# One level of Strassen or two: a float32 factorization kernel on one NeuronCore

## The chip, the core and the metric

The kernel runs on one NeuronCore of one Trainium2 chip. The engines are TensorE (PE in the profile; its weight loads are PEld), VectorE (DVE), ScalarE (ACT), GpSimd (POOL) and SyncE (SP, which here only starts transfers). They work through separate queues, each in order, and wait for one another through semaphores. The metric is device microseconds (us) of the whole program. "The profile" is one execution taken by the hardware profiler; "the page" is its printed summary.

## The reference

`x` is 1024 x 512, the weight is 64 x 512 x 512 (e, f, m), all float32:

```python
out_lin = x @ lin_w.T + lin_b
xv = jnp.einsum('bf,efm->bem', x, weight)
zp = jnp.einsum('bf,efm->bem', jnp.square(x), jnp.square(weight))
interaction = 0.5 * jnp.sum(jnp.square(xv) - zp, axis=1)
return out_lin + interaction
```

The large part is `xv`: a 1024 x 512 matrix times a 512 x 32768 one, of which only the squares, summed over e, are kept. `zp` summed over e needs only the sum over e of the squared weight, one 512 x 512 matrix (`w2_sum`), and one small matrix product.

## The kernel before

The host lays the weight out as 64 column blocks of 512 columns, each with 8 output columns m and all 64 e, so that the sum over e is a sum over 64 neighbours. A block is a 128 x 4 x 512 tile (`w`, 1 MB): 128 partitions, four slices of the contracted dimension.

The kernel multiplies with one level of Strassen (in Winograd's form). The row blocks of `x` and the two halves of the contracted dimension make a 2 x 2 left matrix, `A11` to `A22`; two neighbouring column blocks make the 2 x 2 right matrix. The left sums `S1` to `S4` are made once. For each pair of blocks `column_sums` makes four right sums `t1` to `t4` on VectorE (L124 to L127). Seven products take the place of eight. A product (`product`, L143) is 2 row tiles of 128 rows (`G = 2`) times 2 slices of 128, four matmuls of 128 x 128 by 128 x 512, into a PSUM tile of two banks.

The loop runs over 64 trees: 32 pairs of blocks times two row pieces. The order is written out by hand (`manual_schedule`): products 1, 3, 6, 2, 7, then product 5 of the next tree, then 4. There are four PSUM tiles: `b1`, two `b2`, `b3`. Partial results go on in PSUM: product 1 is copied from `b1` to a `b2` by ScalarE, and products 6, 7 and 4 are added onto it in that bank by TensorE; product 5 is copied out of `b3` as `p5` before product 3 is added onto it, and the sum is copied out as `p53`. Two results need `p53` or `p5` added, by VectorE (L204, L212). Each of the four results of a tree is squared by ScalarE and summed over e by VectorE into `acc` (`finish`, L155 and L156). `squares` (L132, L133) does the same to the weight for `w2_sum`.

All weight loads are on SP's queue. At the start eight matmuls of zeros keep TensorE busy while the first transfers run. At the end, 64 matmuls (L247) make the linear term and the squares' term together, and VectorE adds `acc` and the bias (L252, L255) before the stores.

Of the kernel before, what the change touches and what calls it, by code (L numbers as in the profile page):

```python
# [8 lines left out]
F32 = mybir.dt.float32  # L9
AF = mybir.ActivationFunctionType  # L10
ALU = mybir.AluOpType
AX = mybir.AxisListType


@with_exitstack
def kernel(
# [24 lines left out]

    nc = tc.nc
    NBLK, P, NK, N = weight.shape
    B = xT.shape[1]
    M = out.shape[1]
    MI = M // NBLK
    E = N // MI
    NB = B // P
    H = B // 2
    G = 2  # L50
    NT = H // (G * P)

    const = ctx.enter_context(tc.tile_pool(name="const", bufs=1))
    wpool = ctx.enter_context(tc.tile_pool(name="wpool", bufs=4))
    tpool = ctx.enter_context(tc.tile_pool(name="tpool", bufs=2))
    w2pool = ctx.enter_context(tc.tile_pool(name="w2pool", bufs=1))
    ppool = ctx.enter_context(tc.tile_pool(name="ppool", bufs=2))
    sqpool = ctx.enter_context(tc.tile_pool(name="sqpool", bufs=3))
    opool = ctx.enter_context(tc.tile_pool(name="opool", bufs=2))
    ps1 = ctx.enter_context(  # L60
        tc.tile_pool(name="ps1", bufs=1, space=bass.MemoryType.PSUM)
    )
    ps2 = ctx.enter_context(
        tc.tile_pool(name="ps2", bufs=2, space=bass.MemoryType.PSUM)
    )
    ps3 = ctx.enter_context(
        tc.tile_pool(name="ps3", bufs=1, space=bass.MemoryType.PSUM)
    )
    ctx.enter_context(tc.manual_schedule())

    def psum_tile(kind, name):
        pool = {1: ps1, 2: ps2, 3: ps3}[kind]
        return pool.tile([P, G, N], F32, tag=f"b{kind}", name=f"b{kind}_{name}")

    zero = sqpool.tile([P, N], F32, tag="sq", name="zero")
    nc.vector.memset(zero, 0.0)
    for kind in (1, 2, 2, 3):
        b = psum_tile(kind, f"prime{kind}")
        for j in range(G):
            nc.tensor.matmul(b[:, j, :], zero[:, 0:P], zero, start=True, stop=True)  # L80

    x_src = xT.rearrange("(p k) b -> p k b", k=NK)
    KH = NK // 2

    def const_half(tag):
        return const.tile([P, KH, H], F32, tag=tag, name=tag)

    A = {}
    for h, k, queue in ((0, 0, nc.scalar), (1, 0, nc.scalar), (1, 1, nc.sync), (0, 1, nc.scalar)):
        a = A[h, k] = const_half(f"a{h}{k}")  # L90
        queue.dma_start(a, x_src[:, ts(k, KH), ts(h, H)])

        if (h, k) == (0, 0):
            blocks = {}

            def load(c):
                w = blocks[c] = wpool.tile([P, NK, N], F32, tag="w", name=f"w{c}")
                if c < 2:
                    for q in range(2):
                        nc.sync.dma_start(w[:, ts(q, KH), :], weight[c][:, ts(q, KH), :])  # L100
                else:
                    nc.sync.dma_start(w, weight[c])

            load(0)
            load(1)

    A11, A12, A21, A22 = A[0, 0], A[0, 1], A[1, 0], A[1, 1]
    S1, S2, S3, S4 = (const_half(f"s{i}") for i in range(1, 5))
    lhs = {1: A11, 2: A12, 3: S4, 4: A22, 5: S1, 6: S2, 7: S3}

    acc = const.tile([P, NB, M], F32, tag="acc", name="acc")
    w2_sum = const.tile([P, NK, M], F32, tag="w2_sum", name="w2_sum")

    def column_sums(n):

        w0, w1 = blocks[2 * n], blocks[2 * n + 1]
        b11, b21, b12, b22 = (
            w0[:, 0:KH, :], w0[:, KH:NK, :], w1[:, 0:KH, :], w1[:, KH:NK, :]
        )
        t = {  # L120
            i: tpool.tile([P, KH, N], F32, tag=f"t{i}", name=f"t{i}_{n}")
            for i in range(1, 5)
        }
        nc.vector.tensor_sub(t[1], b12, b11)  # L124
        nc.vector.tensor_sub(t[2], b22, t[1])  # L125
        nc.vector.tensor_sub(t[3], b22, b12)  # L126
        nc.vector.tensor_sub(t[4], b21, t[2])  # L127
        return {1: b11, 2: b21, 3: b22, 4: t[4], 5: t[1], 6: t[2], 7: t[3]}

    def squares(c):  # L130
        w2 = w2pool.tile([P, NK, N], F32, tag="w2", name=f"w2_{c}")
        nc.scalar.activation(w2, blocks[c], AF.Square)  # L132
        nc.vector.tensor_reduce(  # L133
            w2_sum[:, :, ts(c, MI)],
            w2.rearrange("p k (m e) -> p k m e", e=E),
            axis=AX.X,
            op=ALU.add,
        )

    def product(i, rhs, t, b, first):  # L140
        for j in range(G):
            for k in range(KH):
                nc.tensor.matmul(  # L143
                    b[:, j, :],
                    lhs[i][:, k, ts(t * G + j, P)],
                    rhs[i][:, k, :],
                    start=first and k == 0,
                    stop=k == KH - 1,
                    skip_group_check=True,
                )  # L150

    def finish(c, src, h, t, name):

        sq = sqpool.tile([P, G, N], F32, tag="sq", name=f"sq{name}")
        nc.scalar.activation(sq, src, AF.Square)  # L155
        nc.vector.tensor_reduce(  # L156
            acc[:, h * (NB // 2) + t * G:h * (NB // 2) + (t + 1) * G, ts(c, MI)],
            sq.rearrange("p j (m e) -> p j m e", e=E),
            axis=AX.X,
            op=ALU.add,  # L160
        )

    trees = [(n, t) for n in range(NBLK // 2) for t in range(NT)]
    rhs_of = {}
    live = {}

    def open_tree(s):
        n, t = trees[s]
        b3 = psum_tile(3, s)
        product(5, rhs_of[n], t, b3, True)  # L170
        p5 = ppool.tile([P, G, N], F32, tag="p5", name=f"p5_{s}")
        nc.scalar.copy(p5, b3)  # L172
        live[s] = b3, p5

    for s, (n, t) in enumerate(trees):
        name = f"{n}_{t}"
        if s == 0:
            b1 = psum_tile(1, s)
            nc.vector.tensor_sub(S3, A11, A21)
            nc.vector.tensor_add(S1, A21, A22)  # L180
            rhs_of[0] = column_sums(0)
            product(1, rhs_of[0], t, b1, True)
            nc.vector.tensor_sub(S2, S1, A11)
            nc.vector.tensor_sub(S4, A12, S2)
            open_tree(0)
        if t == 0 and n + 1 < NBLK // 2:
            load(2 * n + 2)
            load(2 * n + 3)
        rhs = rhs_of[n]
        b3, p5 = live.pop(s)  # L190

        if s > 0:
            b1 = psum_tile(1, s)
            product(1, rhs, t, b1, True)
        b2 = psum_tile(2, s)
        nc.scalar.copy(b2, b1)  # L196

        product(3, rhs, t, b3, False)
        p53 = ppool.tile([P, G, N], F32, tag="p53", name=f"p53_{s}")
        nc.scalar.copy(p53, b3)  # L200

        product(6, rhs, t, b2, False)
        c12 = ppool.tile([P, G, N], F32, tag="c12", name=f"c12_{s}")
        nc.vector.tensor_add(c12, b2, p53)  # L204

        product(2, rhs, t, b1, False)
        finish(2 * n, b1, 0, t, f"11_{s}")
        finish(2 * n + 1, c12, 0, t, f"12_{s}")

        product(7, rhs, t, b2, False)  # L210
        c22 = ppool.tile([P, G, N], F32, tag="c22", name=f"c22_{s}")
        nc.vector.tensor_add(c22, b2, p5)  # L212
        finish(2 * n + 1, c22, 1, t, f"22_{s}")

        if t == 0:
            squares(2 * n)
            squares(2 * n + 1)
            if n + 1 < NBLK // 2:
                rhs_of[n + 1] = column_sums(n + 1)
        if s + 1 < len(trees):  # L220
            open_tree(s + 1)
        product(4, rhs, t, b2, False)
        finish(2 * n, b2, 1, t, f"21_{s}")

        if s == 1:
            lw_sb = const.tile([P, NK, M], F32, tag="lw", name="lw_sb")
            bias_sb = const.tile([P, M], F32, tag="bias", name="bias_sb")
            nc.gpsimd.dma_start(lw_sb, lin_wT.rearrange("(p k) m -> p k m", k=NK))
            nc.gpsimd.dma_start(bias_sb, lin_b.partition_broadcast(P))
        if s == 3:  # L230
            xq = {}
            for hk, a in A.items():
                xq[hk] = const_half("xq%d%d" % hk)
                nc.vector.scalar_tensor_tensor(xq[hk], a, -0.5, a, ALU.mult, ALU.mult)

    out_dst = out.rearrange("(n p) m -> p n m", p=P)
    kinds = (2, 1, 3, 2)
    for g in range(NB // G):
        ps = psum_tile(kinds[g], f"out{g}")
        o = opool.tile([P, G, M], F32, tag="o", name=f"o{g}")  # L240
        h = g // NT
# [44 lines left out]
```

## Time and profile before

| | |
|---|---|
| median of 3 runs | 1625.71 us (1625.59 to 1626.24) |
| profiled execution | 1625.93 us, its span from first to last instruction 1624.2 us |
| granted TensorE clock | 0.997 |
| TensorE matmuls busy | 1606.1 us, 3728 instructions |
| VectorE / ScalarE / GpSimd busy | 774.5 / 565.7 / 1.4 us |
| HBM traffic | 70.52 MB read, 2.10 MB written |

A busy share is the time in which an engine had an instruction running, over the span. In the page's groups a row names the line, the engine, the operation and the tiles it writes and reads, then the busy time, the mean ns of one instruction, the idle time of the engine just before them and what ended it. "The chain that ended last" goes back from the last instruction to whatever released it, and so on to the start.

### The profile page before, as it was taken

The page shows a single profiled execution, that of the slowest core. Times are in us where ns is not written, and L with a number is a line of the kernel's source. Part 1 is how long each engine was busy: PE and PEld are TensorE (multiplying, and loading weights), DVE is VectorE, ACT ScalarE, POOL GpSimd, SP SyncE. Part 2 cuts the span into 40 slices and gives each one's busy share as a digit, 9 for nine tenths or more (in the row PEclk, how much of TensorE's full clock was granted, in tenths as well). Part 3 has the DMA queues.
Part 4 walks back from the last instruction along what each step waited for, and adds up shares of the span by engine and source line. Part 5 has one row for each costly group of instructions (what it writes and reads, how often), then busy time and mean ns, then how long its engine had stood idle before and what let it go on. Part 6 is the DMA issues. An engine that isn't in the chain of part 4 may idle for free.

```text
span 1624.2 us, 9096 instructions
## 1 busy us (share of the span) xinstructions
PE 1606.1 (99%) x3728; PEld 709.4 (44%) x3728; DVE 774.5 (48%) x601; ACT 565.7 (35%) x513; POOL 1.4 (0%) x6
## 2 busy tenths in 40 slices
PE   7999999999999999999999999999999999999998
PEld 3444444444444444444444444444444444444433
DVE  3556444455444455543445544445544444554421
ACT  1333333343343333333333334333333333333410
POOL 0000000000000000000000000000000000000000
PEclk9999999999999999999999999999999999999999
DMA  4111001111001111101111100111100111110001
GB/s 187 52 52 52 21 31 52 52 52 52 26 26 52 52 52 52 44 19 41 52 52 52 52 26 26 52 52 52 52 34 21 48 52 52 52 52 0 0 13 39
DMA packets 12009, 73.19 MB, mean 45 GB/s; under 512 B 1280, under 2 KB 1280, under 8 KB 3904
## 3 DMA queue, kind: packets, MB, share of 16 engines
q1 hardware_dynamic: 10928, 69.74, 12.0%
q10 hardware_dynamic: 816, 1.57, 0.3%
q0 software_dynamic: 224, 1.31, 0.2%
q8 instruction: 29, 0.48, 0.1%
q14 instruction: 12, 0.10, 0.0%
HBM read 70.52 MB, written 2.10 MB: 45 GB/s over the span
## 4 chain that ended last, share of the span: by engine, by line
PE 98%; DMA 1%; DVE 0%; SPq 0%; issue 0%; ACT 0%; DVEq 0%
PE b L143 95%; PE b_out L247 3%; DMA a<-xT 1%; DVE o L252 0%; SPq L100 0%; DVE c L212 0%; DVE t L124 0%; ACT p L172 0%; DVE o L255 0%; DVE s L180 0%; DVEq L125 0%
## 5 line engine op out<-in xcount | busy, mean ns | idle before, releaser
L143 PE MATMUL b<-t,s 128*128 128x512 f32 x1536 | 682.7, 594 | 6.6 <-DVE t L124 6.6
L156 DVE TENSOR_REDUCE acc<-sq 128x16 f32<-128x1024 f32 x256 | 306.0, 1216 | 419.0 <-ACT sq L155 419.0
L143 PE MATMUL b<-w,a 128*128 128x512 f32 x1024 | 460.3, 592 | 0.0
L143 PEld LDWEIGHTS b<-t,s 128*128 128x128 f32 x1536 | 292.8, 191 | 375.7 <-issue 375.7
L143 PEld LDWEIGHTS b<-w,a 128*128 128x128 f32 x1024 | 194.6, 190 | 244.9 <-issue 244.9
L155 ACT ACTIVATE sq<-b 128x1024 f32<-128x1024 f32 x128 | 131.1, 1024 | 456.1 <-PE b L143 456.1
L143 PE MATMUL b<-t,a 128*128 128x512 f32 x512 | 230.3, 592 | 1.3 <-DVE c L212 1.3
L143 PE MATMUL b<-w,s 128*128 128x512 f32 x512 | 230.3, 592 | 1.1 <-ACT p L172 1.1
L204 DVE TENSOR_TENSOR c<-b,p 128x1024 f32<-128x1024 f32 x64 | 78.3, 1224 | 280.4 <-PE b L143 275.1
L155 ACT ACTIVATE sq<-c 128x1024 f32<-128x1024 f32 x128 | 134.7, 1053 | 176.6 <-DVE c L212 176.6
L133 DVE TENSOR_REDUCE w_sum<-w 128x32 f32<-128x2048 f32 x64 | 146.3, 2286 | 81.8 <-ACT w L132 81.8
L143 PEld LDWEIGHTS b<-t,a 128*128 128x128 f32 x512 | 97.2, 190 | 124.1 <-issue 122.0
L143 PEld LDWEIGHTS b<-w,s 128*128 128x128 f32 x512 | 97.2, 190 | 123.9 <-issue 122.0
L132 ACT ACTIVATE w<-w 128x2048 f32<-128x2048 f32 x64 | 121.7, 1902 | 75.3 <-DVE w_sum L133 75.3
L200 ACT COPY p<-b 128x1024 f32<-128x1024 f32 x64 | 64.8, 1013 | 156.4 <-PE b L143 156.4
L196 ACT COPY b<-b 128x1024 f32<-128x1024 f32 x64 | 63.8, 997 | 74.1 <-PE b L143 72.9
L172 ACT COPY p<-b 128x1024 f32<-128x1024 f32 x64 | 64.1, 1002 | 55.3 <-PE b L143 55.3
L212 DVE TENSOR_TENSOR c<-b,p 128x1024 f32<-128x1024 f32 x64 | 78.4, 1225 | 1.1
L125 DVE TENSOR_TENSOR t<-w,t 128x1024 f32<-128x1024 f32 x32 | 39.2, 1225 | 1.1
L126 DVE TENSOR_TENSOR t<-w 128x1024 f32<-128x1024 f32 x32 | 39.0, 1219 | 0.0
L127 DVE TENSOR_TENSOR t<-w,t 128x1024 f32<-128x1024 f32 x32 | 39.0, 1218 | 0.0
L124 DVE TENSOR_TENSOR t<-w,w 128x1024 f32<-128x1024 f32 x32 | 38.9, 1216 | 0.0
(21 smaller groups left out, 118.2 us busy)
## 6 DMA issues: line engine op xcount, KB each, us to landing
w<-weight SPq DMA_DIRECT2D x62, 1024.0 KB, 4.8
w<-weight SPq DMA_DIRECT2D x4, 512.0 KB, 10.7
out<-o SPq DMA_DIRECT2D x8, 256.0 KB, 2.0
a<-xT ACTq DMA_DIRECT2D x3, 512.0 KB, 12.6
lw_sb<-lin_wT POOLq DMA_DIRECT2D x1, 1024.0 KB, 10.2
a<-xT SPq DMA_DIRECT2D x1, 512.0 KB, 14.8
bias_sb<-lin_b POOLq DMA_DIRECT2D x1, 256.0 KB, 11.5
```

The lines of the kernel that those rows point to most:

```text
L125: nc.vector.tensor_sub(t[2], b22, t[1])
L132: nc.scalar.activation(w2, blocks[c], AF.Square)
L133: nc.vector.tensor_reduce(w2_sum[:, :, ts(c, MI)], w2.rearrange("p k (m e) -> p k m e", e=E), axis=AX.X, op=ALU.add,)
L143: nc.tensor.matmul(b[:, j, :], lhs[i][:, k, ts(t * G + j, P)], rhs[i][:, k, :], start=first and k == 0, stop=k == KH - 1, skip_group_check ...
L155: nc.scalar.activation(sq, src, AF.Square)
L156: nc.vector.tensor_reduce(acc[:, h * (NB // 2) + t * G:h * (NB // 2) + (t + 1) * G, ts(c, MI)], sq.rearrange("p j (m e) -> p j m e", e=E), ...
L172: nc.scalar.copy(p5, b3)
L196: nc.scalar.copy(b2, b1)
L200: nc.scalar.copy(p53, b3)
L204: nc.vector.tensor_add(c12, b2, p53)
L212: nc.vector.tensor_add(c22, b2, p5)
L247: nc.tensor.matmul(ps[:, j, :], lo[h, k // KH][:, k % KH, bt], hi[:, k, :], start=(q == 0), stop=(q == 2 * NK - 1),)
```

## The change

The right matrix now has four column blocks (a group; 16 groups), and Strassen is used twice. The outer level takes the group as 2 x 2 quarters of 256 x 1024 (`w11`, `w12`, `w21`, `w22`, 1 MB each) and the left matrix as four quarters of 512 x 256. The inner level splits each of the seven outer products again. That gives 49 products of 256 x 128 by 128 x 512, two matmuls each, where the kernel before needs 56 products of that size.

- *Left sums.* The seven outer left operands and their inner sums are made once, in `X[1]` to `X[7]`, seven pieces each.
- *Right sums.* The four outer sums of a group (`outer_sum`: `T1`, `T2`, and two written over `w12` and `w21`) are made by VectorE on 2048 columns. The four inner sums of each outer product (`inner_t`) are made by GpSimd on 512 columns.
- *Inner results* are collected in PSUM as before (`b1`, `b2`, `b3`).
- *Outer results* are collected in SBUF tiles (`O1`, `U2`, `U3`), by VectorE as each PSUM tile is read (`outer_psum`, `outer_sbuf`). Where `p5` or `p53` enters too, GpSimd first adds the collected sum to it (`before_sum`). The outer product 5 goes into two results, and there GpSimd does two additions to `U3` and `U2` for each SBUF result.
- *Order.* A tree is one outer product; each group runs its trees in the order 1, 6, 2, 7, 4, 5, 3. Within a tree the inner order is product 1, product 4 of the tree before, 6, 5 of the next tree, 2, 7, 3 of the next tree. The sums over e are put in a queue (`defer`) and emitted in `end_slot` while the VectorE backlog that the program reckons is under a limit; squares are emitted some slots after their result (`at`).
- *Ends.* The linear term is computed first and put in DRAM; each group's partial `acc` goes to DRAM; both come back in the last trees into the weight tiles, which are free then. The priming matmuls are gone. At the end 32 matmuls make the squares' term.

The core of the changed code (the diff replaces nearly the whole body of the kernel function):

```diff
+ORDER = (1, 6, 2, 7, 4, 5, 3)
+SLOT = {1: 0, 7: 1, 2: 2, 4: 3, 5: 4, 6: 5, 3: 6}
...
+    def outer_sum(g, which):
+        t = tiles[g]
+        if which == 1:
+            t["T1"] = full_tile(wpool, "T1", f"T1_{g}")
+            nc.vector.tensor_sub(t["T1"], t["w12"], t["w11"])
+        elif which == 2:
+            t["T2"] = full_tile(wpool, "T2", f"T2_{g}")
+            nc.vector.tensor_sub(t["T2"], t["w22"], t["T1"])
+        elif which == 3:
+            nc.vector.tensor_sub(t["w12"], t["w22"], t["w12"])
+        else:
+            nc.vector.tensor_sub(t["w21"], t["w21"], t["T2"])
+        spend(2.3)
...
+    def inner_t(s, which):
...
+        new = t[which] = tpool.tile([P, N], F32, tag=f"t{which}", name=f"t{which}_{s}")
...
+        nc.gpsimd.tensor_sub(new, a, b)
...
+    def end_slot(limit=1.0):
+        now[0] += 1
+        for fn in later.pop(now[0], ()):
+            fn()
+        while deferred and deferred[0][0] <= now[0]:
+            ready, cost, fn = deferred[0]
+            if busy["dve"] > now[0] + limit and now[0] < ready + 12:
+                break
+            deferred.popleft()
+            spend(cost)
+            fn()
...
+    def product(s, p, b, first):
+        i = trees[s][1]
+        r = rhs(s, p)
+        for j in range(G):
+            nc.tensor.matmul(
+                b[:, j, :], X[i][:, SLOT[p], ts(j, P)], r,
+                start=first, stop=True, skip_group_check=True,
+            )
...
+    def outer_psum(s, b, pos):
+        i = trees[s][1]
+        if i == 1:
+            nc.scalar.copy(target(s, i, pos), b)
+        elif i == 5:
+            nc.vector.tensor_add(U3[pos], U3[pos], b)
+            nc.vector.tensor_add(U2[pos], U2[pos], b)
+            spend(2.44)
+            finish(s, U3[pos], pos, 2)
+        else:
+            other = addend(i, pos)
+            t = target(s, i, pos)
+            nc.vector.tensor_add(t, b, other)
+            spend(1.22)
+            if i in (2, 4, 3):
+                finish(s, t, pos, 2)
+
+    def before_sum(s, p, pos):
+        i = trees[s][1]
+        if i not in (1, 5):
+            nc.gpsimd.tensor_add(p, p, addend(i, pos))
+
+    def outer_sbuf(s, b, p, pos):
+        i = trees[s][1]
+        spend(1.22)
+        if i == 5:
+            nc.vector.tensor_add(p, b, p)
+            nc.gpsimd.tensor_add(U3[pos], U3[pos], p)
+            nc.gpsimd.tensor_add(U2[pos], U2[pos], p)
+            finish(s, U3[pos], pos, 4)
+        else:
+            t = target(s, i, pos)
+            nc.vector.tensor_add(t, b, p)
+            if i in (2, 4, 3):
+                finish(s, t, pos, 2)
...
+    for s in range(last + 1):
+        g, idx = divmod(s, 7)
+        more = g + 1 < NG
+        if s < last:
+            b1s[s] = bank(1, s)
+            product(s, 1, b1s[s], True)
+            b2s[s] = bank(2, s)
+            nc.scalar.copy(b2s[s], b1s[s])
+            before_sum(s, p5[s], 3)
...
+            if idx == 6 and more:
+                outer_sum(g + 1, 2)
+            end_slot()
+        if s > 0:
+            product(s - 1, 4, b2s[s - 1], False)
+            outer_psum(s - 1, b2s[s - 1], 2)
...
+        inner_t(s + 1, 2)
...
+        if idx == 1:
+            outer_sum(g, 3)
+        end_slot()
+        product(s, 6, b2s[s], False)
+        outer_sbuf(s, b2s[s], p53[s], 1)
+        end_slot()
+        first_half(s + 1)
+        inner_t(s + 1, 3)
...
+        end_slot()
+        product(s, 2, b1s[s], False)
+        outer_psum(s, b1s[s], 0)
+        inner_t(s + 1, 4)
...
+        end_slot()
+        product(s, 7, b2s[s], False)
+        outer_sbuf(s, b2s[s], p5[s], 3)
+        if idx == 2:
+            outer_sum(g, 4)
+        if idx == 5 and more:
+            outer_sum(g + 1, 1)
+        end_slot()
+        second_half(s + 1)
+        if s + 1 < last:
+            before_sum(s + 1, p53[s + 1], 1)
+        inner_t(s + 2, 1)
+        end_slot()
```

`first_half(s)` is product 5 into `b3` and ScalarE's copy of it to `p5`; `second_half(s)` is product 3 onto the same bank and the copy to `p53`. `finish` squares a result in place on ScalarE and puts its sum over e in the queue. `spend(c)` is the program's own reckoning of VectorE's time in slots and issues nothing. The loads of the next group's quarters are on SP's queue in the trees with idx 0 (`w22`), 1 (`w11`), 4 (`w12`) and 5 (`w21`).

## The prediction

> **What bounds the kernel now.** I read the page first for busy shares and the chain that ended last, then the chain in order of time for what surrounds the loop, then the groups for prices. The page:
>
> ```profile
> span 1624.2 us, 9096 instructions
> ...
> PE 1606.1 (99%) x3728; PEld 709.4 (44%) x3728; DVE 774.5 (48%) x601; ACT 565.7 (35%) x513; POOL 1.4 (0%) x6
> ...
> PE 98%; DMA 1%; DVE 0%; SPq 0%; issue 0%; ACT 0%; DVEq 0%
> ```
>
> TensorE is on 98% of the chain; VectorE and ScalarE have half their time free, GpSimd does nothing. The chain in order of time:
>
> ```profile
> 20.20 6.14 PE b L143 x8
> ...
> 27.43 1528.11 PE b L143 x3560
> ...
> 1556.85 3.70 PE b L143 x8
> 1560.55 6.88 PE b_out L247 x16
> ```
>
> The second line is one unbroken run: 1528.11/3560 = **0.4292 us per TensorE instruction**. One float32 matmul is two instructions (1792 matmuls in the products, 3584 instructions), so it costs 0.858 us. Everything outside the products: 27.4 us before the long run, less 8 instructions already done, and 63.7 us from 1560.55 to the end, of which 128 x 0.429 = 54.9 is matmul. Prices of the other engines, from the costliest groups:
>
> ```profile
> L156 DVE TENSOR_REDUCE acc<-sq 128x16 f32<-128x1024 f32 x256 | 306.0, 1216 | 419.0 <-ACT sq L155 419.0
> L204 DVE TENSOR_TENSOR c<-b,p 128x1024 f32<-128x1024 f32 x64 | 78.3, 1224 | 280.4 <-PE b L143 275.1
> L133 DVE TENSOR_REDUCE w_sum<-w 128x32 f32<-128x2048 f32 x64 | 146.3, 2286 | 81.8 <-ACT w L132 81.8
> L200 ACT COPY p<-b 128x1024 f32<-128x1024 f32 x64 | 64.8, 1013 | 156.4 <-PE b L143 156.4
> ```
>
> The first row squares' sums, the second adds a PSUM bank to an SBUF tile: both 1.22 us for 1024 columns; 2048 columns take 2.29; a ScalarE pass takes 1.0.
>
> **What the Trainium skill says.** (1) "GPSIMD Engine Reference", section 3.1, measures a float32 tensor_tensor add of 2048 columns at 4497 ns on GpSimd and 2293 on VectorE, about 2.6 cycles of 1.2 GHz per element. The VectorE side agrees with 2286 above; nothing in this trace shows GpSimd arithmetic. (2) "SBUF — State Buffer", section "Who interferes with whom": a VectorE instruction with two SBUF inputs contends with a GpSimd instruction that reads SBUF; with one SBUF input (the other in PSUM, or a reduce) it does not. Not shown here. (3) "TensorE: Matmul & The Clock Gate", Part 1: after an idle window of about 3.4 us TensorE runs at half clock until a busy window has passed. The trace agrees: after a wait of 6.6 us the eight instructions at 20.20 took 6.14 us, where eight warm ones take 3.43.
>
> **The change, part by part.** I call one product (two matmuls, 4 instructions) a slot: 4 x 0.4292 = 1.717 us. A tree is 7 slots (12.02 us), a group of four column blocks 49 slots (84.1 us), and there are 16 groups.
>
> *TensorE.* 64 block products become 49: 16 x 49 x 4 = 3136 instructions x 0.4292 = 1346.1 us, against 3584 and 1538.4: **minus 192.3**. The linear term (32 matmuls, 27.5 us) moves from the end to the start; the squares' matmuls (27.5) stay at the end; the 8 priming matmuls go.
>
> *Start.* The first matmul needs three transfers of 256 KB; at the 346 GB/s that the trace shows in its first 20 us, shared with others in flight, some 5 us. The clock is cold then: plus 2. Linear matmuls 27.5, under which 7 MB arrive (7/0.346 = 20 us), so loads are hidden. Then ScalarE copies stand between products of the first tree with no other tree to cover them (product 5 to 3, product 1 to 6): 1.2 and 1.4 us. First product effectively at 5 + 2 + 27.5 + 2.6 = 37.1 (before: 1560.55 - 1538.4 = 22.1). *End.* 27.5 of matmul, four banks free, then one addition of 0.69 us and the store (3.1 us behind the last VectorE instruction now): 31.3. The 30 small reloads of partial sums on SP's queue start a tree and a half earlier and have that and 27 us; I cost them at nothing, and at 10 if they are late. Floor: 37.1 + 1346.1 + 31.3 = **1414.5** with nothing late.
>
> *VectorE per group.* 28 additions from PSUM x 1.224 = 34.3, 24 reduces x 1.216 = 29.2, 4 outer sums of 2048 columns x 2.29 = 9.2: 72.6 of 84.1 us (86%). Each addition must end before the bank is written again, mostly two slots after: 3.43 us, less 1.4 of its own. The reduces are held back by the emission rule while its reckoned backlog is over one slot. The first group has 28 small sums more (some 10 us) and is full. *ScalarE per group.* 21 copies, 2 more in the first tree, 24 squares: 47 x about 1.02 = 48 us. Where a square lies between the copies after product 3 and product 1: 0.2 + 3 x 0.95 = 3.1 us against the 3.43 at which product 6 is due: fits by 0.3.
>
> *GpSimd per group.* By (1), 60 ns and 2.17 ns a column: 1.17 us for 512 columns, 2.28 for 1024. 28 inner sums = 32.8; 10 additions to p5 or p53 and 4 for tree 5 = 31.9: 64.7 of 84.1. In an ordinary tree its tightest deadline is the inner sum T1 of the next tree: product 3 ends, copy 0.2 + 1.0, addition to p53 2.28, T1 1.17: 4.7 us against the 5.15 (three slots) at which product 5 is due. It fits, with 0.45 to spare.
>
> *Where it does not fit: tree 5 to tree 3.* Time from the start of tree 5. Product 6 ends at 5.15, VectorE's addition at 6.6. GpSimd adds to U3 and U2: 11.15; the two inner sums queued behind: 13.5; the second pair of additions, ready at 12.3: 18.05; the addition to p53 of tree 3: 20.35; T1 of the next group's first tree: 21.5. That T1 is due at 12.02 + 5.15 = 17.17. **TensorE waits 4.35 us**, with every engine's later work behind it. In the same stretch VectorE makes the next group's first two outer sums (4.6 us, two SBUF inputs). By (2) they contend. Full exclusion adds 4.6: 8.9. Shared by the cycle, GpSimd reads two operands in 2.6 cycles (8.0 us of work hold 6.2 of the port), VectorE reads one operand per 0.96 GHz cycle (3.7): 9.9 instead of 8.0, so 6.2 late. I take **6.2**, between 4.35 and 8.9. By (3) a wait over 3.4 us tends to cool the clock: 0.6, **1.8**, 2.7 for the three (the trace's 2.7 as the top, scaled by how surely an idle window falls in the wait). The last group has no successor: 15 x (6.2 + 1.8) = **120 us**.
>
> *Small lateness elsewhere* (outer sum 4 just before T1 of tree 4, ScalarE's 0.3 us): 0 to 2 us per group; I take 0.5: 8.
>
> *SP's queue:* four 1 MB loads per group (4.8 us each) against 84 us; the shortest lead, for w12, is eight slots, 13.7 us. Nothing, while that lead stands. The sums' stores to DRAM wait for the last reduce and hold the next load behind them by a few slots: not due for several trees.
>
> Sum: 1414.5 + 120 + 8 = 1542.5 of span. The execution profiled took 1625.93 for a span of 1624.2, 1.7 more, and lies 0.2 above the median: **1544 us**.
>
> **The rivals.**
> *Slower: the shared port covers the PSUM additions too.* If the one SBUF operand of those 28 additions also comes through the interface that GpSimd uses, 64.7 + 9.2 + 34.3 = 108.2 us per group cannot overlap: 16 x 108.2 + 68.4 = 1800. It decides once the exclusive time passes (1624.2 - 68.4)/16 = 97.2 us a group, that is when 68% of the additions' time is shut out. Against it: the skill's page names two SBUF inputs only. For it: no run here has shown GpSimd reading at all, and the priced work sits at 77% and 86% of two engines side by side.
> *All hidden.* GpSimd is a fifth faster than the page (the 14.9 us from 6.6 to 21.5 shrink to 11.9, 1.4 late) and ports do not collide: 1414.5 + 21 + 1.7 = 1437; with no wait 1416.
> *VectorE becomes the bound.* At 86% by plan, in order, with outer sums of 2.3 us ahead of additions that have 2 us of slack, a bank is late in most trees: 1 us in each of 112 trees on top of 1544 gives some 1650 without recovery, 1600 with half recovered.
> *It does not do what it says:* the compiled order of TensorE has 1568 product matmuls and 64 others, so that is ruled out.
>
> **How the numbers follow.** GpSimd late at each group's end, with contention from none (1414.5 + 15 x 4.95 = 1489) to full (1414.5 + 15 x 11.6 + 16 = 1604): 0.65. All hidden: 0.15. VectorE bound: 0.06. Port covers PSUM additions: 0.14. The range 1425 to 1615 takes the first wholly and most of the second and third. Faster 0.65 + 0.15 + 0.03 = 0.83, slower 0.14 + 0.02 = 0.16, between them 0.01; 0.2% is about what a measurement of this kernel can tell from no change.
>
> **What would show it.** Right: TensorE's product rows busy 1346 us at 0.429 each; GpSimd rows at 1.17 and 2.28 us; among the waits, product instructions on GpSimd's t, longest 5 to 9 us, some 15 times, each followed by a few instructions at half pace; outer sums stretched beyond 2.3 us. Wrong: GpSimd rows far from the page's price; product waits spread over all trees and put down to VectorE (the third rival); VectorE's PSUM additions at 2 us or more in place of 1.22 (the first); a tail over 45 us after the last product (the reloads).

## The result, and the profile after

The changed kernel takes **1674.62 us** (median of 4 runs, 1673.40 to 1675.18) where the kernel before takes 1625.65 (4 runs, 1625.02 to 1626.24): the ratio is 1.03 (95% interval 1.0282 to 1.0318). It is 3% slower; 1544 us and faster had been forecast, with a range that ended at 1615.

The page of the kernel after, its busy shares, the chain that ended last, and the costliest groups (columns as before; "issue" is time in which an engine on the chain waited for nothing that the profile shows):

```profile
span 1672.9 us, 10435 instructions
...
PE 1472.8 (88%) x3264; PEld 634.9 (38%) x3264; DVE 1207.1 (72%) x950; ACT 748.8 (45%) x756; POOL 1187.0 (71%) x677
...
PE 36%; POOL 33%; issue 27%; DVE 3%; ACT 1%; DMA 0%; POOLq 0%; DVEq 0%; SPq 0%
...
L271 PE MATMUL b<-t,X 128*128 128x512 f32 x1792 | 851.1, 614 | 176.6 <-POOL t L238 169.5
...
L345 POOL TENSOR_TENSOR p<-p,oa 128x1024 f32<-128x1024 f32 x96 | 226.9, 2364 | 203.8 <-ACT p L375 203.8
...
L353 POOL TENSOR_TENSOR oa<-oa,p 128x1024 f32<-128x1024 f32 x32 | 106.0, 3313 | 88.6 <-DVE p L352 88.6
```

TensorE has 464 instructions fewer, as forecast, but is on only 36% of the chain. A third of the chain is GpSimd. TensorE's idle time that ends on an inner sum (`t`, GpSimd L238) is 169.5 us. GpSimd's additions come in two kinds: `p<-p,oa` at 2.36 us in the mean, and tree 5's `oa<-oa,p` at 3.31 for the same shape.

One group repeats every 98.93 us ((1522.43 - 137.36)/14, between the first and fifteenth of the long waits below), where its 49 products need 84.13. The timeline of TensorE around the end of one group, then GpSimd's and VectorE's (start, duration, instruction; in brackets the idle time before it and what ended it):

```profile
615.74 3.60 PE L271 MATMUL b<-w,X 128*128 128x512 f32 x8
619.17 3.60 PE L271 MATMUL b<-t,X 128*128 128x512 f32 x8
631.60 3.78 PE L271 MATMUL b<-t,X 128*128 128x512 f32 x4 [8.84 <-POOL t L238]
635.17 3.06 PE L271 MATMUL b<-w,X 128*128 128x512 f32 x4
...
660.49 1.98 PE L271 MATMUL b<-t,X 128*128 128x512 f32 x4 [1.65 <-POOL t L238]
...
685.42 1.98 PE L271 MATMUL b<-t,X 128*128 128x512 f32 x4 [0.63 <-POOL t L238]
```

```profile
612.16 2.35 POOL L353 TENSOR_TENSOR oa<-oa,p 128x1024 f32<-128x1024 f32 x1 [5.27 <-DVE p L352]
614.47 2.39 POOL L354 TENSOR_TENSOR ob<-ob,p 128x1024 f32<-128x1024 f32 x1
616.80 1.29 POOL L238 TENSOR_TENSOR t<-w 128x512 f32<-128x512 f32 x1
618.02 3.33 POOL L238 TENSOR_TENSOR t<-w,t 128x512 f32<-128x512 f32 x1
621.32 4.40 POOL L353 TENSOR_TENSOR oa<-oa,p 128x1024 f32<-128x1024 f32 x1
625.68 2.35 POOL L354 TENSOR_TENSOR ob<-ob,p 128x1024 f32<-128x1024 f32 x1
627.99 2.33 POOL L345 TENSOR_TENSOR p<-p,ob 128x1024 f32<-128x1024 f32 x1
630.29 1.26 POOL L238 TENSOR_TENSOR t<-w 128x512 f32<-128x512 f32 x1
```

```profile
617.62 2.61 DVE L208 TENSOR_TENSOR T<-w,w 128x2048 f32<-128x2048 f32 x1
620.26 3.24 DVE L211 TENSOR_TENSOR T<-w,T 128x2048 f32<-128x2048 f32 x1
```

This is the forecast's own chain, instruction for instruction: two additions, two inner sums, two additions, the addition to `p53`, and then the inner sum that TensorE has waited for since 622.8. The two instructions that overlap VectorE's outer sums take 3.33 and 4.40 us instead of 1.28 and 2.35: each is longer by 2.05 us. After the wait the next four TensorE instructions take 3.57 us from start to start where they take 1.72 at full clock; the chain view gives the whole stretch:

```profile
631.60 15.23 PE b L271 x28
```

28 instructions at 0.4292 are 12.02 us, so the cooled clock costs 3.2 us. Two smaller waits follow, 1.65 and 0.63 us, both on an inner sum that is late by an outer sum: 3 stretches the inner sum itself, 4 the GpSimd addition ahead of it.

### The profile page after: what moved, and what is told of

The parts are those of the page before. It is cut to its first block, busy times and chain, and to the rows that moved or that the text cites. A ratio compares the mean times of both kernels' runs of the same rounds, so it can differ in the third digit from the quotient of the medians.

```text
span 1672.9 us, 10435 instructions
## 1 busy us (share of the span) xinstructions
PE 1472.8 (88%) x3264; PEld 634.9 (38%) x3264; DVE 1207.1 (72%) x950; ACT 748.8 (45%) x756; POOL 1187.0 (71%) x677
## 3 DMA queue, kind: packets, MB, share of 16 engines
HBM read 76.68 MB, written 6.16 MB: 50 GB/s over the span
## 4 chain that ended last, share of the span: by engine, by line
PE 36%; POOL 33%; issue 27%; DVE 3%; ACT 1%; DMA 0%; POOLq 0%; DVEq 0%; SPq 0%
PE b L271 32%; POOL t L238 16%; POOL oa L353 6%; POOL p L345 6%; POOL ob L354 5%; PE b_lin L157 2%; PE b_out L499 2%; DVE oa L358 1%; ACT p L375 1%; DMA lw<-lin_wT 0%; DVE acc L294 0%; DVE lin_all L481 0%; DVE o L503 0%; DVE ob L358 0%; DVE T L211 0%
## 5 line engine op out<-in xcount | busy, mean ns | idle before, releaser
L271 PE MATMUL b<-t,X 128*128 128x512 f32 x1792 | 851.1, 614 | 176.6 <-POOL t L238 169.5
L271 PEld LDWEIGHTS b<-t,X 128*128 128x128 f32 x1792 | 344.5, 195 | 638.2 <-issue 398.7
L271 PE MATMUL b<-w,X 128*128 128x512 f32 x960 | 456.6, 612 | 4.2 <-DVE oa L336 2.1
L345 POOL TENSOR_TENSOR p<-p,oa 128x1024 f32<-128x1024 f32 x96 | 226.9, 2364 | 203.8 <-ACT p L375 203.8
L271 PEld LDWEIGHTS b<-w,X 128*128 128x128 f32 x960 | 190.8, 199 | 251.5 <-issue 244.5
L238 POOL TENSOR_TENSOR t<-w 128x512 f32<-128x512 f32 x160 | 235.6, 1472 | 16.7 <-DMA w<-weight 14.5
L238 POOL TENSOR_TENSOR t<-w,t 128x512 f32<-128x512 f32 x160 | 235.4, 1471 | 1.3
L345 POOL TENSOR_TENSOR p<-p,ob 128x1024 f32<-128x1024 f32 x64 | 165.5, 2586 | 40.6 <-ACT p L375 40.6
L256 DVE TENSOR_REDUCE w_sum<-wsq 128x16 f32<-128x1024 f32 x128 | 154.8, 1210 | 34.8 <-ACT wsq L252 34.8
L271 PE MATMUL b<-T,X 128*128 128x512 f32 x384 | 175.2, 592 | 0.0
L358 DVE TENSOR_TENSOR ob<-b,p 128x1024 f32<-128x1024 f32 x64 | 78.0, 1218 | 84.9 <-POOL p L345 71.2
L358 DVE TENSOR_TENSOR oa<-b,p 128x1024 f32<-128x1024 f32 x96 | 117.2, 1220 | 26.1 <-PE b L271 25.6
L238 POOL TENSOR_TENSOR t<-T,t 128x512 f32<-128x512 f32 x64 | 82.1, 1282 | 59.5 <-PE b L271 58.3
```

Of the source, the lines that this page charges most:

```text
L238: nc.gpsimd.tensor_sub(new, a, b)
L256: nc.vector.tensor_reduce(w2_sum[:, ts(row, KH), m:m + MI], sq.rearrange("p k (m e) -> p k m e", e=E), axis=AX.X, op=ALU.add,)
L271: nc.tensor.matmul(b[:, j, :], X[i][:, SLOT[p], ts(j, P)], r, start=first, stop=True, skip_group_check=True,)
L345: nc.gpsimd.tensor_add(p, p, addend(i, pos))
L358: nc.vector.tensor_add(t, b, p)
```

## The experiments

Theory A: GpSimd's queue around tree 5, lengthened by the port that it shares with VectorE's two-operand sums, and the clock that cools in the wait. Theory B: VectorE's own load, 72% of the span, is the bound. Times beside the expectations are single runs unless a range is given; the kernel before took 1624.96 us beside the first four and 1626.06 (median of 7) beside the others. "Per group" is the mean distance between like waits of TensorE in the timeline, from the first to the fifteenth. The comments in the lines of code below are notes for the reader.

### One operand for the outer sums

```diff
-            nc.vector.tensor_sub(t["T1"], t["w12"], t["w11"])
+            one_input(t["T1"], t["w12"])   # a reduce over groups of one, same length
```

and the same for the other three.

> Each of the four outer sums of a group is replaced by a VectorE pass of the same length over one of its operands (a reduce over groups of one), so it no longer subtracts. Theory A, GpSimd's queue at tree 5 made longer by the shared port: the GpSimd rows that are stretched in the changed kernel (3.3 and 4.4 us for 1.28 and 2.35) return to their plain length, TensorE's wait at the end of each group falls from 8.8 to about 4.8 us, the waits of 1.65 and 0.63 us later in the group go: 15 x 6.4 = 96 us less, and up to 39 more if the clock stays warm: 1540 to 1580. Theory B, VectorE's own load is the bound: these passes shrink from 12.0 to 9.2 us a group, 45 us at most: 1630 or more.

Measured: **1569.95 us**, 92.09 per group. The groups of this run, and TensorE's timeline:

```profile
L358 POOL TENSOR_TENSOR oa<-oa,p 128x1024 f32<-128x1024 f32 x32 | 75.6, 2361 | 88.6 <-DVE p L357 88.6
...
L205 DVE TENSOR_REDUCE T<-w 128x2048 f32<-128x2048 f32 x32 | 71.5, 2277 | 0.0
```

```profile
683.50 3.78 PE L276 MATMUL b<-t,X 128*128 128x512 f32 x4 [4.77 <-POOL t L243]
```

Tree 5's additions are back at 2.36 us, the long wait is 4.77, the two small ones are gone. As A expected; B's most would have been 45 us, and the gain is 104.7. A 4.77 us wait still cools the clock (3.78 us for four).

### Tree 5 without GpSimd's additions

```diff
-            nc.gpsimd.tensor_add(U3[pos], U3[pos], p)
-            nc.gpsimd.tensor_add(U2[pos], U2[pos], p)
```

> GpSimd's four additions of tree 5 (p into U3 and U2) are left out, so two of the four results of each group lack a term. Theory A: the long wait at the end of the group goes, with the slow instructions after it (8.8 + 3.2 us a group), the two small waits stay: 1672.9 - 15 x 12 = about 1490. Theory B (VectorE's load, which is unchanged): over 1640.

Measured: **1552.94 us**, 91.09 per group (single groups 89.9 or 91.6). The gain of 122 us with VectorE's work unchanged contradicts B. But A had been read too simply, and the run missed 1490 by 63: a wait on the same inner sum remained.

```profile
671.11 3.37 POOL L345 TENSOR_TENSOR p<-p,ob 128x1024 f32<-128x1024 f32 x1 [8.29 <-ACT p L373]
674.44 3.32 POOL L238 TENSOR_TENSOR t<-w 128x512 f32<-128x512 f32 x1
```

With the additions gone, the outer sums 1 and 2 ran beside the addition to `p53` and the inner sum itself, which they lengthened by 1.0 and 2.0; TensorE waited 2.69 us. The contention had moved, not gone.

### Matmuls into the wait

```diff
+            if s >= 7 and s % 7 == 0:
+                for n in range(8):
+                    nc.tensor.matmul(
+                        b3s[s][:, n % G, :], X[1][:, 0, ts(n % G, P)],
+                        rhs_tile(s // 7, 1)[:, 0, 0, :],
+                        start=True, stop=True, skip_group_check=True,
+                    )
```

> Eight matmuls more, into the bank that product 5 of each group's first tree overwrites, are put just ahead of that product; they need nothing that is late and last 6.9 us. If the slow instructions after the wait come from a cooled clock: the wait of 8.8 us holds them, 28 instructions after it take 12.0 us again in place of 15.2, and the time falls by 15 x 3.2 = 48 us to some 1627. If their slowness has another cause (a late operand, a queue refilling): no change, 1675. If the fill delays product 5: longer than 1675.

Measured: **1639.41 us**, 96.54 per group. More work in the queue took 35 us off. The timeline:

```profile
611.70 7.03 PE L369 MATMUL b<-w,X 128*128 128x512 f32 x16
620.72 1.98 PE L271 MATMUL b<-t,X 128*128 128x512 f32 x4 [1.99 <-POOL t L238]
```

Four instructions after the wait take 1.98 us, not 3.78, and the mean granted clock of the run is 0.988, not 0.947, so a cooled clock is what made them slow. The gain is 2.4 us per group and not 3.2, in part because the 2.0 us that stay idle still cool it in five of the fifteen groups (2.98 and 2.81 us for four in the first of them and the last); such a group is 1.7 us longer than the others.

### GpSimd's order at tree 5

```diff
         product(s, 6, b2s[s], False)
+        if idx == 5:
+            inner_t(s + 1, 3)
+            inner_t(s + 1, 4)
+            inner_t(s + 2, 1)
         outer_sbuf(s, b2s[s], p53[s], 1)
```

(and not at their old places in that tree).

> Only GpSimd's order at tree 5 changes: the inner sums 3 and 4 of the next tree and 1 of the tree after it are issued ahead of tree 5's additions, into the 5.2 us in which GpSimd waits there for VectorE. Theory A: the first inner sum of the next group is no longer late; late next is product 7 of tree 3, which waits for the addition to p53 behind the four additions, by about 3.8 us with the port contention, with less cooling. 1672.9 - 15 x 7.7 = about 1555. Theory B or any cause outside GpSimd's order: 1670.

Measured: **1584.88 us**, 93.10 per group: the sign and the next wait were right, the size was 30 us short. The wait is now the one named as late next:

```profile
601.02 3.68 PE L271 MATMUL b<-t,X 128*128 128x512 f32 x4 [3.90 <-DVE ob L358]
```

3.90 us for VectorE's addition after `p53`, against 3.8. What was short: the clock still cools in 3.90 us, in each of these groups (3.05 to 3.78 us for four), and the 7.7 of the expectation leaves only some 0.5 us for that.

### Without the sums of the squared weight

```diff
-                def reduce():
...
-                defer(1, 1.22, reduce)
```

> The 128 VectorE reduces that sum the squared weight over e are left out (the sums stay zero), 155 us of VectorE time; the rest is as in the changed kernel. Theory A (GpSimd's queue at tree 5 and the shared port): VectorE has time to spare, 1655 to 1680. Theory B (VectorE's load is the bound): up to 155 us less, about 1520.

Measured: **1640.80 us**, 34 us less: outside A's span by 14 us, and far from B's 1520. The long wait is unchanged and the small one of 1.65 has gone:

```profile
717.07 3.78 PE L262 MATMUL b<-t,X 128*128 128x512 f32 x4 [8.82 <-POOL t L239]
769.44 1.98 PE L262 MATMUL b<-t,X 128*128 128x512 f32 x4 [0.64 <-POOL t L239]
```

With fewer reduces ahead of it outer sum 3 (L213 in the changed kernel, L214 here) ran earlier, at a mean of 2281 ns in place of 3807:

```profile
738.74 2.28 DVE L214 TENSOR_TENSOR w<-w,w 128x2048 f32<-128x2048 f32 x1
740.40 2.82 POOL L336 TENSOR_TENSOR p<-p,oa 128x1024 f32<-128x1024 f32 x1 [8.28 <-ACT p L366]
```

It now starts ahead of GpSimd's addition, which is longer by 0.5 us for it, where in the changed kernel it came behind that addition and then held the inner sum up for 2.0. So 155 us of VectorE's work were worth 34, by where one instruction of each group fell.

### The outer sums moved

```diff
         outer_sbuf(s, b2s[s], p53[s], 1)
+        if idx == 1:
+            outer_sum(g, 3)                  # was a slot earlier
...
         outer_psum(s, b1s[s], 0)
+        if idx == 2:
+            outer_sum(g, 4)                  # was a slot later
+        if idx == 6 and more:
+            outer_sum(g + 1, 1)              # was at tree 5's product 7
...
         outer_sbuf(s, b2s[s], p5[s], 3)
+        if idx == 6 and more:
+            outer_sum(g + 1, 2)              # was at tree 3's product 1
```

> Only the places of the four outer sums in the order change: 3 one slot later, 4 one slot earlier, and the next group's 1 and 2 from tree 5's end and tree 3's begin to behind products 2 and 7 of tree 3. Theory A: the port contention leaves the late additions, what is left of the long wait is GpSimd's own 4.8 us, as with the one-operand passes, and the two small waits go: 1570, up to 1600 if the moved sums make the first inner sum of the second tree late. Theory B: VectorE's work is the same, 1670.

Measured: **1576.21 us**, 92.18 per group, one long wait of 4.75 in each:

```profile
690.51 3.15 PE L271 MATMUL b<-t,X 128*128 128x512 f32 x4 [4.75 <-POOL t L238]
```

The same VectorE instructions in other places give what the one-operand passes gave, with nothing left out.

### Both, and the end

The early inner sums, the moved outer sums, and in tree 3 `inner_t(s + 2, 1)` ahead of `inner_t(s + 1, 3)` and `inner_t(s + 1, 4)`:

> The moved outer sums together with the early inner sums at tree 5, and in tree 3 the inner sum 1 of the second next tree ahead of 3 and 4 of the next. Theory A: with both parts of the lateness gone a group takes its 84.1 us of product time and at most 1 more: 1673 less 15 x 14: about 1460. If one part only stands in for the other: 1570.

Measured: **1501.08 us**, 87.14 per group. The two parts do not stand in for each other: the moved sums alone gave 98 us, the early inner sums 90, together 174. (The change in tree 3 was not run alone; its share of the 174 is not known.) It missed 1460 by 41: a group keeps 3.0 us over its products. VectorE's addition after product 7 of tree 3 now stands behind outer sum 1, and TensorE waits 1.30 us for it:

```profile
665.72 5.76 PE L271 MATMUL b<-t,X 128*128 128x512 f32 x12 [1.30 <-DVE ob L358]
```

The other 1.7 us of a group are in shorter waits, not followed up here. The rest of the miss is in the first group: the moved outer sum 3 and the small sums of `X` run beside GpSimd (outer sum 3 takes 2.68 us there, four sums that take 0.4 alone take 1.4 to 2.6), and TensorE waits 6.16 us. The end was as before.

```diff
                     start=(k == 0), stop=(k == NK - 1),
                 )
-            nc.vector.tensor_add(o[:, j, :], ps[:, j, :], tail["lin", h][:, r, :])
+        for j in range(G):
+            h, r = divmod(g * G + j, NB // 2)
+            nc.vector.tensor_add(o[:, j, :], ps[:, j, :], tail["lin", h][:, r, :])
```

and `x` squared behind products 2 and 7 of the last tree.

> As the kernel with both, and at the end: all matmuls of an output pair are issued ahead of its two additions, and the two squarings of x move from tree 5's end to behind products 2 and 7 of the last tree. Against that kernel: 9 us of waits between output matmuls and some 6 us in the last tree go, 15 in all: about 1445.

Measured: **1487.75 us** (4 runs, 1487.31 to 1488.44), 13 less than the kernel with both, where 15 were expected. That the sizes agree is in part luck. The output matmuls gave more than their 9: from the first of them to the end it is 33.4 us instead of 46.0, because the waits between them went and with them the slow clock after the first. The last tree gave nothing: the squarings moved there now stand ahead of an addition that TensorE waits for, and its two waits are 1.61 and 4.73 us, where they were 3.65 and 1.39.

```profile
1448.89 3.78 PE L276 MATMUL b<-t,X 128*128 128x512 f32 x4 [4.73 <-DVE ob L363]
```

The level, 1445, was not reached for the reasons given for the kernel with both. Against the kernel before the ratio is **0.9151** (0.9136 to 0.9166): 8.5% faster. Its page:

```profile
PE 1431.5 (96%) x3264; PEld 613.4 (41%) x3264; DVE 1171.4 (79%) x950; ACT 750.6 (51%) x756; POOL 1113.1 (75%) x677
...
PE 75%; DVE 12%; POOL 6%; issue 6%; DMA 0%; DVEq 0%; SPq 0%
```

TensorE is back on 75% of the chain. VectorE and GpSimd do the same work as in the kernel that was 3% slower.

## Why the prediction was wrong

The path and its cause were forecast; the sign was wrong because terms that were each named were mostly each too small, and together they outweigh the products saved. Against the execution profiled (span 1672.9):

| term | predicted | measured |
|---|---|---|
| start, up to the products, with the first group's waits | 37.1 | 49.5 |
| products | 1346.1 | 1346.1 |
| long wait, 15 times | 6.2 each, 93 | 8.84 each, 132.6 |
| clock and small waits, per group | 1.8 + 0.5, 35 in all | 5.96 (83.4 for 14 groups), and 16.4 in the last |
| end | 31.3 | 44.7 |
| sum | 1542.5 | 1672.7 |

The start is 137.36, the end of the first long wait, less that wait and 46 products (79.0); the end runs from 1628.17, after the last product.

- **What bounds it** was right: the product instructions cost 0.4292 us, loads were hidden, and the chain from tree 5 to the next group's first inner sum is the bound, each group. Leaving out its additions, making it shorter and reordering it all moved the time; taking 155 us from VectorE did so only by the shift of one instruction.
- **GpSimd's prices** were close: 1.28 us for 1.17, 2.36 for 2.28, 4 to 9% over the estimates made from the Trainium skill's "GPSIMD Engine Reference", section 3.1. They account for only 0.4 us of the lateness: without contention it was 4.77 where 4.35 was forecast.
- **The step that failed first is the choice of 6.2 us** between 4.35 and 8.9. It was reached by letting the two engines share the port by the cycle. Of the shared ports "SBUF — State Buffer", "Who interferes with whom", says "it's an exclusive lock", and the runs agree: 2.05 us onto a GpSimd instruction for each outer sum of 2.28. That is the upper bound of the text, 8.9, measured at 8.84: 40 us. That the two meet so closely is in part luck: GpSimd alone was 0.4 us later than forecast, and the two outer sums added 4.1 us in place of 4.6.
- **The clock** was mis-sized next. 1.8 us had been taken, from a half-clock state entered only by chance in a wait of that length; it came in every group and cost 3.2, above the 2.7 of the upper end. Then the small waits: 0.5 had been allowed, 1.65 + 0.63 = 2.28 came, and each of the three waits costs 0.1 to 0.2 more than its length (5.96 less 3.2 and 2.28). The text did name outer sum 4 as close to the inner sum of tree 4. It had outer sum 3 nowhere, whose 3.81 us for a planned 2.29 belongs to the larger of the two waits. The last group lost 16.4, where only the small waits had been put down: besides the slow clock and the two small waits, TensorE waits 5.12 and 1.39 us in the last tree. The 5.12 are a chain through GpSimd's additions of tree 5, one of which took 4.42 us beside the squaring of `x` (two SBUF operands, 3.89 us where its second takes 2.28). Together these are 65 us.
- **The start** was 12 us short. The first matmul waited until 7.39 (5 forecast). In the first group VectorE's 256-column sums for `X`, 0.43 us with GpSimd idle, average 1.12 on one line: two SBUF operands again, and the load that the text called full was reckoned with uncontended durations. How the rest of the 12 divides was not tried.
- **The end** was 13 us short. "Four banks free" overlooked that an output pair's second four matmuls wait for the addition of the first four: 0.78 us three times, and 5.74 for the first, whose addition stood in VectorE's queue behind the output sums and three reduces. After that wait the clock is cooled too: 16 instructions take 9.92 us, 7.13 in the next pairs. The chain ran through it:

```profile
1630.05 4.21 DVE lin_all L481 x2
1634.26 3.39 DVE acc L294 x3
...
1638.83 9.94 PE b_out L499 x16
```

- **The reloads and SP's queue** were costed at nothing, rightly: no product waits on a load.
- **The rivals.** "The shared port covers the PSUM additions too" would have been slower for a reason that is not there: `L358 DVE ... oa<-b,p` has a mean of 1220 ns with GpSimd busy 71% of the time, against 1224 before. "VectorE becomes the bound" is contradicted by the runs above. The slower side was reached by the likeliest case's own mechanism, whose range had been cut at 1615: its own upper ends for each term gave 1604, and the start, the end and the clock lay above them.

## What to carry to other kernels

A queue's average load (GpSimd at 77%, VectorE at 86% by plan) did not tell whether a kernel fits; the deadline of each instruction in the fullest stretch did, and there the same work in another order was worth 174 us. Before sums go to GpSimd, list which VectorE instructions have two SBUF operands, and put each where GpSimd either has nothing to do or has nothing that is soon due. Where a wait falls on TensorE, count the clock's recovery with it: here some 3 us after each wait of 4.7 to 8.8 us (a group's 92.09 less 84.13 and the wait of 4.77 in the run with one operand leaves 3.2; the changed kernel's 28 instructions give 3.2 as well).

## What the runs showed of the hardware

TensorE's clock cooled in shorter waits than expected. The Trainium skill ("TensorE: Matmul & The Clock Gate", Part 1) speaks of an idle window of about 3.4 us. Here waits of 1.9 to 2.7 us were at times enough, and at times not, while none of the waits of 1.6 to 1.7 us was (1.98 or 1.99 us for four each time). The shortest that cooled it is one of 1.88 us in the run with one operand (3.12 us for four). From the run without tree 5's additions, the same wait in two groups:

```profile
130.04 3.65 PE L271 MATMUL b<-t,X 128*128 128x512 f32 x4 [2.68 <-POOL t L238]
...
677.82 1.98 PE L271 MATMUL b<-t,X 128*128 128x512 f32 x4 [2.69 <-POOL t L238]
```

Why one cooled and the other didn't was not tried. In that run, from 404.76 us on, the time of the four instructions repeats every three groups (1.98, some 3.2, some 2.6), while the wait stays at 2.68 or 2.69; so the length of the wait alone does not decide it.

And GpSimd and VectorE shut each other out for whole instructions, both ways, where VectorE's instruction has two SBUF operands. Outer sum 3 in the changed kernel:

```profile
654.81 2.35 POOL L345 TENSOR_TENSOR p<-p,oa 128x1024 f32<-128x1024 f32 x1 [8.28 <-ACT p L375]
657.12 3.31 POOL L238 TENSOR_TENSOR t<-w 128x512 f32<-128x512 f32 x1
```

```profile
655.40 3.91 DVE L213 TENSOR_TENSOR w<-w,w 128x2048 f32<-128x2048 f32 x1
```

It starts under GpSimd's addition, which keeps its length, and ends 2.15 us after it, about the 2.28 that it takes alone; the inner sum that starts next is then longer by 2.0, and ends 1.1 us after the outer sum. In the mean outer sum 3 took 3.81 us, and the GpSimd instructions beside outer sums were longer by up to 2.05, nearly a whole outer sum. With one operand (2277 ns) neither was longer.
